# A fused graph-attention layer: the first group's start reordered, head 0's sums called earlier

## The chip, the cores and the metric

The kernel runs on one core of one Trainium2 chip. The metric is the device time of one execution in microseconds, median of several; the profile is that of one execution. The engines are TensorE (PE, matrix products), VectorE (DVE), ScalarE (ACT), GpSimd (POOL) and SyncE (SP); each works through its own queue in order (e1 below moves one instruction in VectorE's queue, and the gap behind it goes). A scheduler, not the program text alone, fixes these orders when the kernel is built: it moves an instruction forward when it believes that its operands are ready.

## The reference, cut to what matters

```python
h = relu(layernorm(x))                     # x: 128 graphs x 64 nodes x 512
# first attention, 4 heads: W_heads[h] 512x512, a_heads[h] 1024
f1, f2 = (h @ W[h]) @ a1[h], (h @ W[h]) @ a2[h]      # "scores"
att = softmax(mask(leaky(f1[:, None] + f2[None, :])))
h1[h] = elu(att @ (h @ W[h]))
# second attention, one head: W_out 2048x512, then a feed-forward layer
o = elu(att2 @ (concat(h1) @ W_out))
y = layernorm(relu(o @ w1 + b1) @ w2 + b2 + o)
out = x + y
```

All in float32. 8192 rows are worked in 16 groups of 512 rows (4 tiles of 128).

## The kernel before: the parts concerned

The 512x512 products are done by a seven-product scheme in place of eight: operand blocks are added and subtracted first ("sums"), and seven products of 256-wide blocks follow (`p` = 1 to 7), whose results are combined by VectorE into `t`, `s15` and the four output blocks. The weights' sums are made once, by GpSimd, and stored in DRAM (`tc`); the data's sums are made for every head and group.

```python
def weight_sums(m):                        # before; m: 4 W_heads, 4 blocks of W_out, w1, w2
    w = MT.pop(m)
    ...
    nc.gpsimd.tensor_tensor(s[0][:, 0], b12, b11, ALU.subtract)          # L202
    nc.gpsimd.tensor_tensor(s[0][:, 1], b22, s[0][:, 0], ALU.subtract)   # L203
    nc.gpsimd.tensor_tensor(s[1][:, 0], b22, b12, ALU.subtract)          # L204
    nc.gpsimd.tensor_tensor(s[1][:, 1], b21, s[0][:, 1], ALU.subtract)   # L205
    ... nc.gpsimd.dma_start(out=TC[m][i], in_=s[i])                      # L208, i = 0, 1

def unit(name, product, post, order): ...
    # after product p: 1 -> s (ScalarE copies the bank), 6 -> t, 5 -> s15 (VectorE, L251);
    # products 7, 3 and 4 add to the banks of 6, 5 and 6, so 7 waits for t, 3 for s15

def scores2(g):                            # second attention's scores, group before
    for j in range(G):                     # 4 tiles x 2: eight products on VectorE, "jf" (L611)
        for c in range(2):
            nc.vector.scalar_tensor_tensor(junk, WH2[g][:, j], 1.0, ao[:, c, :], ..., accum_out=f[...])
    ...

# start-up: fold each head's a into its W (wa = W a), so that scores need no projection
for m in range(FH): fold_dve(m, ab[m])     # heads 0, 1 on VectorE
for m in range(FH, H): fold_pe(m, aT, pw)  # heads 2, 3 on TensorE
...
project_f(0); scores1(0); attn_weights(0 and 1)     # pf, L; s1pe; softmax (L397 to L416)
for m in range(len(mats)): ... weight_sums(m)       # all ten, on GpSimd
run(attend1(0))                            # attention of group 0 (pz, z)
...
for g in range(NG):                        # first projection of g, beside scores2 ... of g - 1
    ...                                    # second projection of g, beside attention of g + 1
```

In the profile, `g_a` is a bank of the first projection, `g_b` of the second, `g_c` and `g_d` of the feed-forward layer. `L` is what ScalarE makes of the folded scores `pf`, `s1pe` the scores of the first attention, `s1e` and `s1A` its softmax, `z` the attention's result, `zs_z` its sums. Line numbers are those of each kernel's own text: the helper of the products `g_a` is L284 before and L300 after, that of `t_a` is L251 and L267, the softmax's subtraction is L404 and L420.

## Time and profile before

| | before |
|---|---|
| device time, median of 3 | 2433.73 us (2433.13 to 2437.04) |
| span of the profiled execution, mean granted clock | 2432.8 us, 0.988 |
| TensorE busy | 2344.2 us, 96% |
| `L` made; softmaxes of the first group | 50.53; 55.13 to 71.74 |
| first product of `g_a` | 81.27 |
| first product of the second projection | 148.79 |
| first product of the next group | 213.16 |

The times are microseconds from the span's start. A timeline line reads: start, duration, engine, line of the text, operation, what it writes <- what it reads, sizes, count; the bracket at its end is the time for which the engine sat idle before it, and what ended that.

### The profile page before, as it was taken

To read this page: it belongs to the slowest core of one execution; us is meant where nothing else is said; L and a number is where in the kernel's file an instruction comes from. 1 tells how busy PE (TensorE), PEld (TensorE's weight loads), DVE (VectorE), ACT (ScalarE), POOL (GpSimd) and SP (SyncE) were. 2 spreads that over 40 slices of the span, in tenths; PEclk is the share of its full clock that TensorE was granted. 3 is DMA by queue.
4 is the path that set the end of the run, shared out by engine and by line. 5 is a ranking of instruction groups with operands and counts; after the bars stand their busy time and mean duration, and the time that the engine had idled before them with its cause. 6 is when DMAs were issued, how large, how long until landed. Compare 5 with 4: busy or idle time off the path is not lost.

```text
span 2432.8 us, 33084 instructions
## 1 busy us (share of the span) xinstructions
PE 2344.2 (96%) x11849; PEld 1961.4 (81%) x11849; DVE 1451.6 (60%) x2468; ACT 787.1 (32%) x1386; POOL 1020.0 (42%) x863
## 2 busy tenths in 40 slices
PE   5799999999999999999999999999999999999997
PEld 4588888888888888888888888888888888888885
DVE  6655565574755647565574755647566574744637
ACT  1342415233251432415233251432415234141412
POOL 6742443534444253443434444253442534433334
PEclk9899999999999999999999999999999999999999
DMA  8644454454544445454454544445454454534542
GB/s 295 235 137 137 129 165 134 139 172 130 169 128 150 157 133 171 130 165 142 135 169 129 168 130 149 156 132 171 130 161 141 135 169 131 164 124 146 166 146 98
DMA packets 260498, 369.00 MB, mean 152 GB/s; under 512 B 22344, under 2 KB 145256, under 8 KB 260336
## 3 DMA queue, kind: packets, MB, share of 16 engines
q1 hardware_dynamic: 252176, 345.92, 44.3%
q10 hardware_dynamic: 5280, 10.49, 1.4%
q0 software_dynamic: 2880, 10.49, 1.1%
q8 instruction: 95, 1.56, 0.3%
q14 instruction: 67, 0.55, 0.1%
HBM read 339.54 MB, written 27.26 MB: 151 GB/s over the span
## 4 chain that ended last, share of the span: by engine, by line
PE 92%; DVE 2%; issue 2%; POOL 2%; DMA 2%; ACT 0%; SPq 0%; DVEq 0%; POOLq 0%; ACTq 0%
PE g_b L299 32%; PE g_a L284 32%; PE g_c L284 8%; PE g_d L299 8%; PE pz L499 4%; PE pa L642 2%; PE pzS L499 1%; PE pto L669 1%; PE pth L348 1%; PE s1pt L449 1%; DMA pw<-in_L_gnn_W_out_dram 1%; PE s1pe L383 1%; PE pf L358 1%; DMA pw<-in_L_gnn_w_dram 0%; DMA aj<-in_adj_dram 0%
## 5 line engine op out<-in xcount | busy, mean ns | idle before, releaser
L299 PE MATMUL g_b<-w,h 128*128 128x256 f32 x2560 | 603.8, 381 | 0.0
L299 PEld LDWEIGHTS g_b<-w,h 128*128 128x128 f32 x2560 | 476.6, 190 | 74.1 <-issue 14.4
L284 PE MATMUL g_a<-zs_z,w 128*128 128x256 f32 x1536 | 376.7, 395 | 41.4 <-issue 31.5
L284 PEld LDWEIGHTS g_a<-zs_z,w 128*128 128x128 f32 x1536 | 304.0, 199 | 98.7 <-issue 43.9
L284 PE MATMUL g_a<-z,w 128*128 128x256 f32 x1536 | 363.1, 379 | 0.0
L284 PEld LDWEIGHTS g_a<-z,w 128*128 128x128 f32 x1536 | 291.6, 190 | 53.0 <-issue 14.7
L299 PE MATMUL g_b<-w,hS 128*128 128x256 f32 x1024 | 243.5, 384 | 0.0
L561 POOL TENSOR_TENSOR hS<-hS,h 128x512 f32<-128x512 f32 x64 | 81.9, 1279 | 384.1 <-DVE hS L523 379.1
L299 PEld LDWEIGHTS g_b<-w,hS 128*128 128x128 f32 x1024 | 189.5, 190 | 38.6 <-issue 10.0
L588 POOL TENSOR_TENSOR h<-h,h 128x512 f32<-128x512 f32 x64 | 81.2, 1270 | 237.7 <-PE g_b L299 237.7
L522 ACT ACTIVATE exc<-exc 128x512 f32<-128x512 f32 x256 | 161.0, 629 | 6.6
L523 DVE SCALAR_TENSOR_TENSOR h<-exc,h 128x512 f32<-128x512 f32 x128 | 107.3, 838 | 62.5 <-ACT exc L522 62.4
L588 POOL TENSOR_TENSOR h<-hS,h 128x512 f32<-128x512 f32 x64 | 81.2, 1269 | 140.1 <-PE g_b L299 138.4
L521 ACT ACTIVATE exc<-h 128x512 f32<-128x512 f32 x128 | 80.7, 631 | 177.4 <-DVE h L558 177.1
L311 POOL TENSOR_TENSOR zs_z<-z,zs_z 128x512 f32<-128x512 f32 x63 | 85.9, 1364 | 111.4 <-PE g_a L284 111.4
L309 POOL TENSOR_TENSOR zs_z<-zS,z 128x512 f32<-128x512 f32 x63 | 89.2, 1417 | 93.0 <-PE g_a L284 72.8
L299 PE MATMUL g_d<-w,rt 128*128 128x256 f32 x512 | 122.5, 382 | 1.8 <-DVE n2ve L324 1.1
L284 PE MATMUL g_c<-ot,w 128*128 128x256 f32 x512 | 121.9, 381 | 0.0
L284 PE MATMUL g_a<-zS,w 128*128 128x256 f32 x512 | 121.1, 379 | 0.0
L310 POOL TENSOR_TENSOR zs_z<-z,zs_z 128x512 f32<-128x512 f32 x63 | 80.2, 1274 | 79.9 <-PE g_d L299 62.1
L299 PEld LDWEIGHTS g_d<-w,rt 128*128 128x128 f32 x512 | 95.9, 190 | 20.5 <-issue 5.2
L284 PEld LDWEIGHTS g_a<-zS,w 128*128 128x128 f32 x512 | 96.0, 190 | 19.0 <-issue 7.4
(155 smaller groups left out, 3659.5 us busy)
## 6 DMA issues: line engine op xcount, KB each, us to landing
w<-tc SPq DMA_DIRECT2D x640, 256.0 KB, 2.7
w<-in_L_gnn_W_heads_dram SPq DMA_DIRECT2D x192, 256.0 KB, 2.8
w<-in_L_gnn_W_out_dram SPq DMA_DIRECT2D x192, 256.0 KB, 2.8
w<-in_L_gnn_w_dram SPq DMA_DIRECT2D x96, 256.0 KB, 2.7
x<-in_x_dram SPq DMA_DIRECT2D x66, 256.0 KB, 2.9
xr<-in_x_dram SPq DMA_DIRECT2D x64, 256.0 KB, 2.9
out_dram<-o SPq DMA_DIRECT2D x64, 256.0 KB, 2.4
tc<-pt POOLq DMA_DIRECT2D x20, 512.0 KB, 6.8
```

What stands on the lines that cost most here:

```text
L284: nc.tensor.matmul(bk[:, o, :], w[:, k, ts(o, P)], a[:, k, :], start=start and o == 0 and k == 0, stop=k == 1, skip_group_check=True,)
L299: nc.tensor.matmul(bk[:, j, :], a[:, k, ts(j, P)], w[:, k, :], start=start and k == 0 and j == 0, stop=i == len(ms) - 1 and k == 1, skip_g ...
L309: eng.tensor_tensor(s2, s1, a11, ALU.subtract)
L310: eng.tensor_tensor(s4, a12, s2, ALU.subtract)
L311: eng.tensor_tensor(s3, a22, s2, ALU.subtract)
L499: nc.tensor.matmul(banks[b][:, c, :].rearrange("p (h n) -> p h n", h=H), src[rows, off + c * P:off + (c + 1) * P], at[rows, b], start=True ...
L521: nc.scalar.activation(ex, src, AF.Relu, scale=-1.0)
L522: nc.scalar.activation(ex, ex, AF.Exp, scale=-1.0)
L523: nc.vector.scalar_tensor_tensor(dst, ex, -1.0, src, ALU.add, ALU.max)
L561: nc.gpsimd.tensor_tensor(dst, dst, H1["22"][:, h], ALU.add)
L588: nc.gpsimd.tensor_tensor(dst[:, h], x0[:, h], x1[:, h], ALU.subtract)
L642: nc.tensor.matmul(pa, AT2[g][:, j, :], WH2[g][:, j, :], start=True, stop=True)
```

## The change

Its title names two things. Head 0's sums of the next group are called during the second projection, in place of at the start of the first. And the first group is rearranged: three heads are folded on VectorE and one on TensorE; the weight sums of heads 0 to 3 come before the softmaxes and all others after them; the sums of W_heads 0 and 1 are read from where GpSimd makes them ("DIRECT") and not by way of DRAM; two products come before the second half of the attention. The mask work on VectorE moves behind the first statistics, and `n1nb`, a small step of the normalisation, moves from VectorE to GpSimd.

```diff
-    homes = ("h11", "h22", "h12", "wh2", "out", "wh2", "out", "wh2", "out", "wh2")
+    homes = ("h11", "h22", "h12", "wh2", "out", "wh2", "out", "wh2", "out", "out")
+    stages = ("ot", "rt", "out", "hS", "ot", "rt", "ot", "rt", "ot", "rt")
...
-    def weight_sums(m):
+    def weight_sums(m, after=None):
...
+        first = nc.gpsimd.tensor_tensor(s[0][:, 0], b12, b11, ALU.subtract)
+        if after is not None:
+            tc.add_manual_dep(first.ins, after.ins.name, ...)
...
-        nc.vector.scalar_tensor_tensor(nb, mean, -1.0, rstd, ALU.mult, ALU.mult)
+        nc.gpsimd.tensor_scalar(nb, mean, rstd, -1.0, ALU.mult, ALU.mult)
...
-            z_sums(g, 0)
...
-    for m in range(FH):
-        fold_dve(m, ab[m])
-    for m in range(FH, H):
-        fold_pe(m, aT, pw)
+    fold_dve(0, ab[0])
+    fold_dve(1, ab[1])
+    fold_pe(2, aT)
+    fold_dve(3, spread_a(3))
+    for m in range(H):
+        weight_sums(m)
     project_f(0)
...
-    for m in range(len(mats)):
-        if m >= H:
-            fetch(m)
-        weight_sums(m)
-    run(attend1(0))
+    attn = attend1(0)
+    for fn in attn[:4]:
+        fn()
+    head0 = project1(0, 0)
+    for fn in head0[:2]:
+        fn()
+    transpose_weights(1)
+    for fn in attn[4:]:
+        fn()
+    z_sums(0, 0)
...
+            side = stage_a(1)
+            for i, m in ((6, 4), (11, 5), (16, 6), (21, 7)):
+                side.insert(i, lambda m=m: more_sums(m))      # fetch(m), weight_sums(m, softmax_end)
...
+            tr, ff, fin = [], [lambda: more_sums(M1), lambda: None, lambda: more_sums(M2), load_rows], []
...
+            early = [lambda: z_sums(g + 1, 0)]
+            at = 8 if g >= 1 else 0
+            run(project2(g), mix(attn, tr) + mix(ff[:at] + early + ff[at:], stage_a(g + 2)) + fin)
```

More of the change, by code (lines that the diff above doesn't have):

```diff
@@ L94, in load @@
         return tl
-    for t in range(G):
+    X[0] = load(0)
+    ar = wk.tile([2 * H, O], FP, tag="elu", name="ar", bufs=3)
+    nc.sync.dma_start(out=ar, in_=a_heads.rearrange("h (r p) -> (h r) p", p=O))
+    for t in range(1, G):
         X[t] = load(t)
+    ah = wk.tile([2 * H * KC, P], FP, tag="elu", name="ah", bufs=3)
+    nc.sync.dma_start(out=ah, in_=a_heads.rearrange("h (r p) -> (h r) p", p=P))
     aj = const.tile([P, N], mybir.dt.int32, name="aj")
@@ L101, in gat_preln_kernel, with masks @@
     negm = const.tile([P, N], FP, name="negm")
-    nc.vector.tensor_scalar(negm, aj, 0.0, None, ALU.is_gt)
-    nc.vector.tensor_scalar(negm, negm, NEG, -NEG, ALU.mult, ALU.add)
     blkones = const.tile([P, NB, N], FP, name="blkones")
-    nc.vector.memset(blkones, 0.0)
-    for b in range(NB):
-        nc.vector.memset(blkones[ts(b, N), b, :], 1.0)
     eye = const.tile([P, N], FP, name="eye")
-    nc.vector.tensor_add(eye, ident[:, 0:N], ident[:, N:2 * N])
-    id32 = const.tile([P, 32], FP, name="id32")
-    nc.vector.tensor_reduce(id32, ident.rearrange("p (j r) -> p r j", r=32), AX.X, ALU.add)
     headrow = const.tile([P, H], FP, name="headrow")
-    nc.vector.tensor_add(headrow, id32[:, 0:H], id32[:, H:2 * H])
     isf = const.tile([P, 2], FP, name="isf")
-    nc.vector.tensor_reduce(isf, id32[:, 0:2 * H].rearrange("p (c h) -> p c h", c=2), AX.X, ALU.add)
     isq = const.tile([P, 2, 2], FP, name="isq")
-    for q in range(2):
-        par = sm.tile([P, 1], FP, tag="par", name=f"par{q}")
-        nc.vector.tensor_reduce(
-            par, ident.rearrange("p (a q r) -> p q a r", a=2, q=2)[:, q], AX.XY, ALU.add
-        )
-        nc.vector.tensor_scalar(isq[:, q], isf, par, None, ALU.mult)
+    wa = const.tile([P, KC, 32], FP, name="wa")
+    def masks():
+        nc.vector.memset(wa, 0.0)
+        id32 = const.tile([P, 32], FP, name="id32")
+        nc.vector.tensor_reduce(id32, ident.rearrange("p (j r) -> p r j", r=32), AX.X, ALU.add)
+        nc.vector.tensor_add(headrow, id32[:, 0:H], id32[:, H:2 * H])
+        nc.vector.tensor_reduce(isf, id32[:, 0:2 * H].rearrange("p (c h) -> p c h", c=2), AX.X, ALU.add)
+        for q in range(2):
+            par = sm.tile([P, 1], FP, tag="par", name=f"par{q}")
+            nc.vector.tensor_reduce(
+                par, ident.rearrange("p (a q r) -> p q a r", a=2, q=2)[:, q], AX.XY, ALU.add
+            )
+            nc.vector.tensor_scalar(isq[:, q], isf, par, None, ALU.mult)
+        nc.vector.memset(blkones, 0.0)
+        for b in range(NB):
+            nc.vector.memset(blkones[ts(b, N), b, :], 1.0)
+        nc.vector.tensor_scalar(negm, aj, 0.0, None, ALU.is_gt)
+        nc.vector.tensor_scalar(negm, negm, NEG, -NEG, ALU.mult, ALU.add)
+        nc.vector.tensor_add(eye, ident[:, 0:N], ident[:, N:2 * N])
     mats = [W_heads[h] for h in range(H)]
@@ L130, in gat_preln_kernel @@
     M1, M2 = 2 * H, 2 * H + 1
-    homes = ("h11", "h22", "h12", "wh2", "out", "wh2", "out", "wh2", "out", "wh2")
+    homes = ("h11", "h22", "h12", "wh2", "out", "wh2", "out", "wh2", "out", "out")
+    stages = ("ot", "rt", "out", "hS", "ot", "rt", "ot", "rt", "ot", "rt")
     MT, TC = {}, {}
-    wa = const.tile([P, KC, 32], FP, name="wa")
-    nc.vector.memset(wa, 0.0)
+    DIRECT = {}
     def fetch(m):
@@ L138, in fetch, with spread_a @@
         nc.scalar.dma_start(out=MT[m], in_=mats[m].rearrange("(k p) o -> p k o", p=P))
-    FH = 2
-    def load_a():
-        ar = wk.tile([2 * H, O], FP, tag="elu", name="ar", bufs=3)
-        nc.sync.dma_start(out=ar, in_=a_heads.rearrange("h (r p) -> (h r) p", p=O))
-        rows = H * 2 * KC
-        ah = wk.tile([rows, P], FP, tag="elu", name="ah", bufs=3)
-        nc.sync.dma_start(out=ah, in_=a_heads.rearrange("h (r p) -> (h r) p", p=P))
-        return ar, ah
-    def spread_a(ar, m):
+    def spread_a(m):
         ab = []
@@ L162, in spread_a, with turn_a @@
         return ab
-    def turn_a(ah):
+    def turn_a():
         rows = H * 2 * KC
@@ L167, in turn_a @@
         nc.tensor.transpose(pt, ah, ident[0:rows, 0:rows])
-        aT = const.tile([P, H, 2, KC], FP, name="aT")
+        aT = wk.tile([P, H, 2, KC], FP, tag="s1", name="aT")
         nc.scalar.copy(aT.rearrange("p h c o -> p (h c o)"), pt)
@@ L180, in fold_dve, with fold_pe @@
                 )
-    def fold_pe(m, aT, pw):
+    def fold_pe(m, aT):
+        pw = aux([P, KC, 2], "pwa")
         for k in range(KC):
@@ L191, in fold_pe @@
                 nc.tensor.matmul(
-                    pw[:, k, :, m - FH], wT[:, o, :], aT[:, m, :, o],
-                    start=(m == FH and k == 0 and o == 0), stop=(o == KC - 1), skip_group_check=True,
-                )
-    def weight_sums(m):
+                    pw[:, k, :], wT[:, o, :], aT[:, m, :, o],
+                    start=(k == 0 and o == 0), stop=(o == KC - 1), skip_group_check=True,
+                )
+        nc.scalar.copy(wa[:, :, m:m + H + 1:H], pw)
+    def weight_sums(m, after=None):
         w = MT.pop(m)
@@ L199, in weight_sums @@
         b21, b22 = w[:, 2:4, 0:Q], w[:, 2:4, Q:O]
-        tag = ("ot", "rt")[m % 2]
-        s = [big.tile([P, 2, 2, Q], FP, tag=f"{tag}{i}", name=f"pt{m}_{i}") for i in range(2)]
-        nc.gpsimd.tensor_tensor(s[0][:, 0], b12, b11, ALU.subtract)
+        tag = stages[m]
+        if tag[1] == "t":
+            s = [big.tile([P, 2, 2, Q], FP, tag=f"{tag}{i}", name=f"pt{m}_{i}") for i in range(2)]
+        else:
+            both = big.tile([P, 2, 2, 2, Q], FP, tag=tag, name=f"pt{m}")
+            s = [both[:, 0], both[:, 1]]
+        first = nc.gpsimd.tensor_tensor(s[0][:, 0], b12, b11, ALU.subtract)
+        if after is not None:
+            tc.add_manual_dep(
+                first.ins, after.ins.name,
+                mybir.DependencyInfo(mybir.DependencyClass.Sync, mybir.DependencyReason.DATA),
+                reason="the sums do not disturb VectorE before",
+            )
         nc.gpsimd.tensor_tensor(s[0][:, 1], b22, s[0][:, 0], ALU.subtract)
@@ L208, in weight_sums @@
             nc.gpsimd.dma_start(out=TC[m][i], in_=s[i])
+        if m < 2:
+            for p, i in ((5, 0), (6, 1), (7, 2), (4, 3)):
+                DIRECT[m, p] = s[i // 2][:, i % 2]
     def piece(m, p):
+        if (m, p) in DIRECT:
+            return DIRECT.pop((m, p))
         w = ring.tile([P, 2, Q], FP, tag="w", name=f"w{m}_{p}")
@@ L415, in softmax @@
             )
-            nc.vector.tensor_copy(A[:, :, H], A[:, :, 0])
+            LAST["A"] = nc.vector.tensor_copy(A[:, :, H], A[:, :, 0])
             return A
@@ L433, in softmax @@
         return A
-    A1, E1 = {}, {}
+    A1, E1, LAST = {}, {}, {}
     def attn_weights(p):
@@ L540, in project1 @@
         z = ZB[g]
+        first = (g, h) == (0, 0)
         if h == 0:
@@ L544, in project1 @@
                 H1[b] = big.tile([P, H, 2, T], FP, tag=tag, name=f"h{b}_{g}")
-            z_sums(g, 0)
-        s2, s3, s4 = ZSUM[h]
-        blk = {1: z["11"][:, h], 2: z["12"][:, h], 3: s4, 4: z["22"][:, h],
-               5: z["S1"][:, h], 6: s2, 7: s3}
+        sums = {6: 0, 7: 1, 3: 2}
+        blk = {1: "11", 2: "12", 4: "22", 5: "S1"}
         def post(what, a, b=None):
@@ L561, in post @@
                 nc.gpsimd.tensor_tensor(dst, dst, H1["22"][:, h], ALU.add)
-        s = unit(f"a{g}_{h}", product_t(h, lambda p: blk[p]), post, (1, 6, 5, 2, 7, 3, 4))
+        s = unit(
+            f"a{g}_{h}", product_t(h, lambda p: ZSUM[h][sums[p]] if p in sums else z[blk[p]][:, h]),
+            post, (1, 2, 6, 5, 7, 3, 4) if first else (1, 6, 5, 2, 7, 3, 4),
+        )
         def next_sums():
@@ L726, in mix @@
     def mix(*lists):
+        lists = [l for l in lists if l]
         keyed = [((i + 0.5) / len(l), n, fn) for n, l in enumerate(lists) for i, fn in enumerate(l)]
         return [fn for _, _, fn in sorted(keyed, key=lambda k: k[:2])]
-    ar, ah = load_a()
     for m in range(H):
@@ L736, in gat_preln_kernel @@
         norm1(t)
-    ab = [spread_a(ar, m) for m in range(FH)]
-    aT = turn_a(ah)
+    masks()
+    ab = {m: spread_a(m) for m in (0, 1)}
+    aT = turn_a()
     for t in range(G):
         transpose_h(t)
-    for m in range(FH):
-        fold_dve(m, ab[m])
-    pw = aux([P, KC, 2, H - FH], "pwa")
-    for m in range(FH, H):
-        fold_pe(m, aT, pw)
-    for c in range(2):
-        nc.vector.tensor_copy(wa[:, :, c * H + FH:(c + 1) * H], pw[:, :, c])
+    fold_dve(0, ab[0])
[4 more added lines that the diff above has]
+        weight_sums(m)
     project_f(0)
@@ L751, in gat_preln_kernel @@
         attn_weights(p)
-    for p in range(2):
-        transpose_weights(p)
-    for m in range(len(mats)):
-        if m >= H:
-            fetch(m)
-        weight_sums(m)
-    run(attend1(0))
+    softmax_end = LAST["A"]
+    transpose_weights(0)
+    attn = attend1(0)
[8 more added lines that the diff above has]
+    z_sums(0, 0)
     ao = const.tile([P, 2, FO], FP, name="ao")
@@ L763, in gat_preln_kernel, with load_rows, more_sums @@
     bs = const.tile([P, FO], FP, name="bs")
-    rows = [(ao[:, 0, :], a_out[0:FO]), (ao[:, 1, :], a_out[FO:2 * FO]), (b2s, b2), (gs, gamma), (bs, beta)]
-    for dst, src in rows:
-        nc.sync.dma_start(out=dst, in_=src[None, :].to_broadcast([P, FO]))
     b1s = const.tile([P, DF // P], FP, name="b1s")
-    for d in range(DF // P):
-        nc.sync.dma_start(out=b1s[:, d:d + 1], in_=b1[ts(d, P)][:, None])
+    def load_rows():
+        rows = [(ao[:, 0, :], a_out[0:FO]), (ao[:, 1, :], a_out[FO:2 * FO]), (b2s, b2), (gs, gamma), (bs, beta)]
+        for dst, src in rows:
+            nc.sync.dma_start(out=dst, in_=src[None, :].to_broadcast([P, FO]))
+        for d in range(DF // P):
+            nc.sync.dma_start(out=b1s[:, d:d + 1], in_=b1[ts(d, P)][:, None])
+    def more_sums(m):
+        fetch(m)
+        weight_sums(m, softmax_end)
     for t in range(G, 2 * G):
@@ L773, in gat_preln_kernel @@
     for g in range(NG):
-        heads = [fn for h in range(H) for fn in [lambda h=h: steps.extend(project1(g, h))]]
-        side = stage_e(g - 1) if g >= 1 else stage_a(1)
-        steps, n = [], 6 * H
-        done = 0
+        if g >= 1:
+            side = stage_e(g - 1)
+        else:
+            side = stage_a(1)
+            for i, m in ((6, 4), (11, 5), (16, 6), (21, 7)):
+                side.insert(i, lambda m=m: more_sums(m))
+        done, n = 0, 6 * H
         for i in range(n):
             if i % 6 == 0:
-                heads[i // 6]()
-            steps[i]()
+                steps = head0 if (g, i) == (0, 0) else project1(g, i // 6)
+            if (g, i // 2) != (0, 0):
+                steps[i % 6]()
             while done * n < (i + 1) * len(side):
@@ L789, in gat_preln_kernel @@
         else:
-            tr, ff, fin = [], [], []
+            tr, ff, fin = [], [lambda: more_sums(M1), lambda: None, lambda: more_sums(M2), load_rows], []
         if g < NG - 1:
-            tail = mix(ff, stage_a(g + 2)) if ff or g + 2 < NG else []
-            run(project2(g), mix(attn, tr) + tail + fin if attn or tr else tail + fin)
-        else:
-            held = 2
-            run(project2(g), tr + [lambda: None] * 6 + ff[:held])
-            left = ff[held:]
-            run(left, [
+            early = [lambda: z_sums(g + 1, 0)]
+            at = 8 if g >= 1 else 0
+            run(project2(g), mix(attn, tr) + mix(ff[:at] + early + ff[at:], stage_a(g + 2)) + fin)
+        else:
+            run(project2(g), tr + [lambda: None] * 6 + ff[:2])
+            run(ff[2:], [
                 lambda: scores2(g), lambda: None, lambda: None, lambda: None, lambda: softmax2(g),
```

## The prediction

> **What bounds the kernel now.** I read the page's busy shares first, then its 40 slices, then the list of waits of TensorE, then the timeline around the places where it waits.
>
> ```profile
> PE 2344.2 (96%) x11849; PEld 1961.4 (81%) x11849; DVE 1451.6 (60%) x2468; ACT 787.1 (32%) x1386; POOL 1020.0 (42%) x863
> PE   5799999999999999999999999999999999999997
> PEclk9899999999999999999999999999999999999999
> ```
>
> TensorE is busy 2344.2 of 2432.8 us; 88.6 us are idle. A slice is 60.8 us: the first two, at 5 and 7 tenths, hold about half of that, the rest is spread thinly. So two things can be won: the start-up, and small gaps that come back in every group. The change takes no product away. The waits, largest first, name both:
>
> ```profile
> PE g_a L284 <- issue: 31.5, 14, 3.5
> PE pab L158 <- DMA ar<-in_L_gnn_a_heads_dram: 12.7, 1, 12.7
> PE s1pt L449 <- DVE s1A L412: 10.7, 2, 9.4
> PE g_a L284 <- DVE t_a L251: 7.8, 1, 7.8
> ```
>
> The columns are total, times, longest. The first line is one gap of about 2.2 us at the start of each of the last 14 groups. The title of the change suggests that these are waits for head 0's sums (L309 to L311 on GpSimd). The timeline at one of them says otherwise:
>
> ```profile
> 347.37 1.26 POOL L311 TENSOR_TENSOR zs_z<-z,zs_z 128x512 f32<-128x512 f32 x1
> ...
> 363.26 0.68 DVE L320 BATCH_NORM_STATS2 n1st<-x 128x6 f32<-128x512 f32 x1
> 364.19 0.68 DVE L251 TENSOR_TENSOR t_a<-g_a,s_a 128x512 f32<-128x512 f32 x1
> 364.97 5.38 PE L284 MATMUL g_a<-zs_z,w 128*128 128x256 f32 x16 [2.28 <-issue]
> ```
>
> The last sum of head 0 ended at 348.63, before the group's first product at 355.62. TensorE started again 0.10 us after VectorE's t_a (364.19 + 0.68 = 364.87). At the gaps near 511, 656 and 802 us it is again 0.10 us. t_a stood in VectorE's queue behind scores2's eight products (L611) and a normalisation, solid work since 342.93.
>
> The start-up in order of time:
>
> ```profile
> 57.96 4.05 DVE L404 TENSOR_TENSOR s1e<-s1e,s1mx 128x512 f32<-128x512 f32 x1
> 65.98 0.69 DVE L403 TENSOR_REDUCE s1mx<-s1e 128x8 f32<-128x512 f32 x1
> 81.27 1.99 PE L284 MATMUL g_a<-z,w 128*128 128x256 f32 x8
> 88.61 4.36 DVE L310 TENSOR_TENSOR zs_z<-z,zs_z 128x512 f32<-128x512 f32 x1
> 98.20 3.78 PE L284 MATMUL g_a<-zs_z,w 128*128 128x256 f32 x8 [7.85 <-DVE t_a L251]
> ```
>
> Folding ends at 48.4, scores reach VectorE at 55.1, the two softmaxes end at 71.7, the first product is at 81.3, TensorE is steadily full from about 118, and the second projection starts at 148.95. The 4.05 and 4.36 us operations are of a kind that takes about 0.7 elsewhere; GpSimd was then subtracting weights (1.26 us an operation).
>
> **What the Trainium skill says.** "SBUF — State Buffer", section Who interferes with whom: VectorE operations with two SBUF inputs share a read port with GpSimd, held for the whole instruction; the other side blocks. The trace agrees: 4.05 us against 0.92 for L404 of the second softmax; reductions stay at 0.69. "TensorE: Matmul & The Clock Gate", section Architectural detail, says ScalarE and VectorE queues are strict FIFO; t_a behind scores2 agrees, and it will matter for ScalarE below. The same page, section What's actually happening, says an idle array falls to half clock; granted clock was 0.66 at 90 to 100 us, and the product at 98.20 (x8: four matmuls in two passes) took 3.78, twice the usual 1.89 us.
>
> **The change part by part.**
>
> *Steady groups: 0 us.* I built both programs and compared the order on each engine. GpSimd's order per group is the same except for four n1nb that move to it from VectorE (about 0.5 us each at n1rs's length; on VectorE about 0.16). Head 0's sums stand where they stood: the scheduler had already moved them up. VectorE's 95 instructions around the boundary keep their order; t_a remains behind scores2. TensorE's feed-forward products move by one place among the second projection's. So I expect the 14 gaps to remain, near 31 us. The removed n1nb lie beside the products.
>
> *Folding: −8.5 us.* VectorE's mask work now comes after the statistics; six of these operations each cost one GpSimd operation of 1.26 us, from about 13.5 when the mask lands, so folding starts near 21 (before: 22.55). Twenty-four folds at 0.61 us (23.16 to 23.77 is one) are 14.7, ending near 36 instead of 48.4; TensorE has one head to turn, not two, and isn't last. But the new buffers give part back: W_out's first block (home "out") takes the buffer in which head 2's sums are staged, so ScalarE, in order, issues that load ahead of L only after those sums were stored. GpSimd gets to that store near 34.3; stores take 6.8 us (page, median), more in this crowded time: L near 42, before 50.53.
>
> *Softmax undisturbed: −5.6 us.* 55.13 to 71.74 is 16.6. Without GpSimd's subtractions one takes seven operations at 0.72, two short ones at 0.22 to 0.24 and ScalarE's 0.63, less overlap: about 5.5, two are 11.0.
>
> *Products before the second half of attention, sums of heads 0 and 1 read where they are made: −11 us.* From the softmax's end to the end of the next group's pf, with nine products done, the kernel before took 111.5 − 71.7 = 39.8. Followed through the new queues at the durations above, the first product comes some 2 us after the softmax rather than 9.5, the 7.85 wait goes (the zs operations no longer meet a train of weight sums), and a wait of about 5 us comes in its place while the evictions of zS and z22 stand behind the first elu: about 29.
>
> *Weight sums of heads 4 to 7 during the first projection: +9.4 us.* Their loads stand in ScalarE's queue, each waiting for GpSimd to finish the previous block in the same buffer: block 4 done after head 0's last product (near 87 on the new clock), block 6 landing 8 us later (the chain of before shows such loads at 7.9 to 10.3), four subtractions of 1.26, then the load of w1, 8 more, then the end of block 5 before block 7's load may start. While ScalarE waits, s1 copies, Exp and elus wait, and VectorE behind them. I get TensorE waits of 3.6 at head 2's second product, 1.3 at a later one and 6.3 at head 3's second; the kernel before had 1.8 there. 11.2 − 1.8 = 9.4. The last blocks are stored near 137 and needed near 150, so the second projection isn't held up.
>
> Sum: −8.5 −5.6 −11 +9.4 = −15.7. 2433.7 − 15.7 = 2418.0 us.
>
> **The rivals.** (a) The gaps go too: if the moved feed-forward products let VectorE reach t_a 2 us earlier, 31 us more are won and the time is about 2387. For it: VectorE waited for TensorE before 342.93. Against: the order of its last 95 instructions is the same, and so are the products that it waits for. (b) ScalarE's queue doesn't hold TensorE up, because loads land in 5 us when fewer stores run: the 9.4 vanish, 2408. For it: ScalarE is only 32% busy. Against: it is in order, and the loads wait on GpSimd, not on bytes. (c) The start is bound by bytes: 300 to 390 GB/s until 50 us, and the new order brings seven weight pieces forward; x6 and x7 then come late for VectorE's queue ahead of the scores, or the stores of block 2 take 10 us or more. Folding's gain falls to 3 and later loads slip: about 2427. (d) The last weights come too late for the second projection: up to 10 us more, 2428.
>
> **Range and chances.** Nothing in 2280 us of steady groups should move; all uncertainty is in the first 150 us, where the gain lies between 5 and 29. Range 2405 to 2429. Faster by over 2% needs 48.7 us, which only (a) with a full start-up gain gives: 3%. Slower by 2%: 1%. Within: 96%.
>
> **What will show it.** First product of g_a near 60 (before 81.3); L404 near 0.7; the second projection's first product near 133 (before 148.95); ScalarE idle behind loads of W_out near 91 to 100 and 103 to 115, with TensorE gaps at s1's heads 2 and 3; 14 gaps of about 2 us still there, each 0.1 us after a t_a. I'm wrong if those gaps are gone, or if the second projection starts before 122 or after 144.

## The result, and the profile after

| | before | after |
|---|---|---|
| device time, median | 2434.19 us (2433.13 to 2437.04, 4 runs) | 2413.73 us (2407.63 to 2418.43, 4 runs) |
| ratio, 95% interval | | 0.9913 (0.9889 to 0.9937): within 2% |
| span of the profiled execution, clock | 2432.8 us, 0.988 | 2411.1 us, 0.984 |

Every ratio in this text is the mean time of one kernel's fast runs over the mean of the other's fast runs of the same rounds, so it is not quite the ratio of the medians.

First the page of the changed kernel: busy time of each engine, and TensorE's busy share and granted clock in 40 slices of 60.3 us.

```profile
PE 2331.4 (97%) x11805; PEld 1949.1 (81%) x11805; DVE 1433.7 (59%) x2418; ACT 782.5 (32%) x1383; POOL 1051.0 (44%) x927
...
PE   6899999999999999999999999999999999999997
...
PEclk7999999999999999999999999999999999999999
```

The second slice went from 7 to 8 tenths busy; the rest of TensorE's line looks as before. The first digit of the clock fell from 9 to 7: the granted clock was 0.73 from 20 to 30 us and 0.50 from 30 to 55, where the folding of one head on TensorE (29.02 to 36.01) and both softmaxes lie. The waits of TensorE name what is left (total, times, longest):

```profile
PE g_a L300 <- issue: 29.1, 14, 3.2
PE g_a L300 <- ACT s_a L265: 10.8, 2, 6.3
```

The 14 gaps at the group boundaries are still there: 29.1 us against 31.5. The second line is new. One of the gaps, in the timeline:

```profile
345.99 0.68 DVE L336 BATCH_NORM_STATS2 n1st<-x 128x6 f32<-128x512 f32 x1
...
346.60 0.40 DVE L635 TENSOR_TENSOR s2dg<-eye,f 128x256 f32<-128x256 f32 x1
346.92 0.68 DVE L267 TENSOR_TENSOR t_a<-g_a,s_a 128x512 f32<-128x512 f32 x1
...
347.70 5.38 PE L300 MATMUL g_a<-zs_z,w 128*128 128x256 f32 x16 [1.96 <-issue]
```

`t_a` ended at 347.60, TensorE went on 0.10 us later, as before. It stood behind the same work: scores2's products, a normalisation, `s2dg`. The sums of this group's head 0 were finished at 331.68 (GpSimd's last of them started at 330.42 and took 1.26 us), 16 us ahead of the gap. So the call that the title names first had nothing to take away there.

The sixteen matmuls after this gap took 5.38 us, at a granted clock of 0.50 from 349 to 351 us; sixteen at full clock take 3.69. The granted clock isn't the same after every gap: the slow form follows 11 of the 14 gaps in the profile of before and 9 of 14 in that of after. Adding gap and slow part, before spends 31.5 + 18.2 us at the boundaries and after 29.1 + 16.1; the difference of 4.5 us is nearly all of what the two traces differ by beyond the start. (From the next group's first product to the end: before 2432.8 − 213.16 = 2219.6, after 2411.1 − 196.20 = 2214.9.)

The start, from the timeline:

```profile
38.81 0.46 ACT L380 ACTIVATE L<-pf,isq 128x128 f32<-128x128 f32 x1 [2.59 <-POOL pt L216]
...
45.64 0.69 DVE L420 TENSOR_TENSOR s1e<-s1e,s1mx 128x512 f32<-128x512 f32 x1
...
56.64 1.97 PE L300 MATMUL g_a<-z,w 128*128 128x256 f32 x8
...
101.31 0.37 ACTq L147 DMA_DIRECT2D pw<-in_L_gnn_w_dram  x1
101.73 0.63 ACT L421 ACTIVATE s1e<-s1e 128x512 f32<-128x512 f32 x1 [10.91 <-POOL pt L216]
...
103.40 3.47 PE L300 MATMUL g_a<-z,w 128*128 128x256 f32 x8 [6.26 <-ACT s_a L265]
```

`L` comes 11.7 us earlier, the softmax's subtraction takes 0.69 us in place of 4.05, the first product comes 24.6 us earlier. Then something is given back: ScalarE issued the load of w1 at 101.31 and had stood idle for 10.91 us before its next operation, until GpSimd had finished the block in the same buffer; `s_a` waited behind it, and TensorE 6.26 us for `s_a`. The same happens again 19 us later (12.55 and 4.56 us). In stages, each worked out from the times at which it starts and ends:

| stage (us) | before | after | difference | predicted |
|---|---|---|---|---|
| start to `L` | 50.53 | 38.81 | −11.7 | −8.5 |
| `L` to the softmax | 4.60 | 4.66 | +0.1 | 0 |
| two softmaxes | 16.61 | 11.46 | −5.1 | −5.6 |
| softmax's end to nine products done | 39.8 | 27.0 | −12.8 | −11 |
| from there to the second projection | 37.3 | 50.3 | +13.0 | +9.4 |
| second projection's first product | 148.79 | 132.23 | −16.6 | −15.7 |

### The profile page after: what moved, and what is told of

It is laid out like the page before. It is cut to its first block, busy times and chain, and to the rows that moved or that the text cites. A ratio compares the mean times of both kernels' runs of the same rounds, so it can differ in the third digit from the quotient of the medians.

```text
span 2411.1 us, 32917 instructions
## 1 busy us (share of the span) xinstructions
PE 2331.4 (97%) x11805; PEld 1949.1 (81%) x11805; DVE 1433.7 (59%) x2418; ACT 782.5 (32%) x1383; POOL 1051.0 (44%) x927
## 4 chain that ended last, share of the span: by engine, by line
PE 93%; POOL 2%; issue 2%; DVE 1%; DMA 1%; ACT 0%; ACTq 0%; SPq 0%; DVEq 0%; POOLq 0%
PE g_b L315 33%; PE g_a L300 31%; PE g_d L315 8%; PE g_c L300 8%; PE pz L515 4%; PE pa L660 2%; PE pzS L515 1%; PE pto L687 1%; PE s1pt L465 1%; PE pth L364 1%; PE s1pe L399 1%; PE pf L374 1%; DMA pw<-in_L_gnn_W_out_dram 0%; POOL pt L216 0%; POOL pt L207 0%
## 5 line engine op out<-in xcount | busy, mean ns | idle before, releaser
L300 PE MATMUL g_a<-zs_z,w 128*128 128x256 f32 x1504 | 364.9, 393 | 29.1 <-issue 29.1
L300 PE MATMUL g_a<-z,w 128*128 128x256 f32 x1520 | 362.0, 381 | 11.4 <-ACT s_a L265 10.8
L300 PEld LDWEIGHTS g_a<-zs_z,w 128*128 128x128 f32 x1504 | 295.6, 197 | 84.0 <-issue 41.8
L606 POOL TENSOR_TENSOR h<-h,h 128x512 f32<-128x512 f32 x64 | 86.8, 1356 | 225.2 <-PE g_b L315 225.2
L327 POOL TENSOR_TENSOR zs_z<-z,zs_z 128x512 f32<-128x512 f32 x63 | 85.9, 1363 | 108.9 <-PE g_a L300 108.9
L326 POOL TENSOR_TENSOR zs_z<-z,zs_z 128x512 f32<-128x512 f32 x63 | 85.2, 1353 | 91.7 <-PE g_d L315 73.8
```

The lines of the kernel that those rows point to most:

```text
L300: nc.tensor.matmul(bk[:, o, :], w[:, k, ts(o, P)], a[:, k, :], start=start and o == 0 and k == 0, stop=k == 1, skip_group_check=True,)
L326: eng.tensor_tensor(s4, a12, s2, ALU.subtract)
L327: eng.tensor_tensor(s3, a22, s2, ALU.subtract)
L606: nc.gpsimd.tensor_tensor(dst[:, h], x0[:, h], x1[:, h], ALU.subtract)
```

## The experiments

Each was timed beside the kernel before on one chip. "gaps" is the line "g_a <- issue" of TensorE's waits, mostly the boundaries; the next group's first product is a clean measure of the start, as the kernels with an unchanged start show: 196.20 after, 196.17, 195.28 and 196.04 in e1, e3 and e5.

| run | median us | before there | ratio (95%) | second projection | next group | gaps |
|---|---|---|---|---|---|---|
| e1 | 2392.68 | 2435.97 | 0.9818 (0.9805 to 0.9831) | 131.61 | 196.17 | 2.9 |
| e2 | 2410.04 | 2435.97 | 0.9894 (0.9881 to 0.9906) | 147.78 | 212.16 | 1.9 |
| e3 | 2420.28 | 2435.97 | 0.9933 (0.9922 to 0.9945) | 131.31 | 195.28 | 30.9 |
| e4 | 2422.19 | 2435.97 | 0.9941 (0.9929 to 0.9953) | 119.81 | 198.44 | 32.8 |
| e5 | 2370.47 | 2439.69 | 0.9715 (0.9701 to 0.9730) | 132.07 | 196.04 | 1.1 |
| e6 | 2410.74 | 2439.69 | 0.9885 (0.9869 to 0.9901) | 118.58 | 182.56 | 34.6 |
| e7 | 2419.64 | 2439.69 | 0.9918 (0.9901 to 0.9934) | 134.83 | 198.81 | 33.2 |
| e8 | 2414.43 | 2439.69 | 0.9898 (0.9877 to 0.9919) | 127.44 | 191.65 | 35.4 |
| e9 | 2360.54 | 2439.92 | 0.9675 (0.9661 to 0.9690) | 120.51 | 184.48 | 2.3 |
| e10 | 2449.25 | 2439.92 | 1.0041 (1.0026 to 1.0056) | 157.80 | 222.18 | 39.2 |
| e11 | 2430.45 | 2439.92 | 0.9969 (0.9952 to 0.9986) | 139.75 | 203.73 | 31.1 |
| e12 | 2429.91 | 2439.92 | 0.9962 (0.9947 to 0.9977) | 137.93 | 201.90 | 35.9 |

### What makes the 14 gaps: e1, e2, e3, e5

**e1: t_a goes first.** The call alone can't be moved, since the scheduler puts scores2 where its operands are ready; a dependency is needed.

```diff
-            [lambda: scores2(g)] + gap * 6 + ...
+            gap * 3 + [lambda: scores2(g, TA[6])] + gap * 3 + ...      # TA[6]: t_a of the next group's head 0
...                                                                     # in scores2, for (j, c) == (2, 0):
+                    tc.add_manual_dep(jf.ins, after.ins.name, ...)     # products of tiles 2, 3 wait for t_a
```

> The changed kernel, with the second half of scores2's products (tiles 2 and 3) told to wait for t_a of the next group's head 0, so that t_a goes first in VectorE's queue. Theory (the 14 gaps are t_a standing behind scores2): they go, all or nearly all of 29.1 us, and with them most of the slow sixteen matmuls after a gap (5.38 us instead of 3.69 in 10 of 14 groups, some 17 us); 2414 becomes about 2372, between 2362 and 2390. Rival (the gaps are waits for the sums of head 0 on GpSimd, as the title has it, or any wait of TensorE's own): unchanged, 2409 to 2419.

The gaps went from 29.1 to 2.9 us, as the theory has it, and the rival is out. But the time fell to 2392.7 and not to 2372, outside the range given: a new wait had come. First TensorE's waits of e1, then its timeline:

```profile
PE g_a L300 <- DVE s_a L267: 16.6, 13, 1.5
...
PE g_a L300 <- issue: 2.9, 5, 0.8
```

```profile
358.83 1.89 PE L300 MATMUL g_a<-zs_z,w 128*128 128x256 f32 x8
...
360.22 0.69 DVE L443 TENSOR_TENSOR s2A<-s2e,s2rb 128x512 f32<-128x512 f32 x1
360.83 0.69 DVE L539 SCALAR_TENSOR_TENSOR hS<-exc,hS 128x512 f32<-128x512 f32 x1
361.43 0.68 DVE L267 TENSOR_TENSOR s_a<-g_a,s_a 128x512 f32<-128x512 f32 x1
...
362.17 1.99 PE L300 MATMUL g_a<-zs_z,w 128*128 128x256 f32 x8 [1.45 <-DVE s_a L267]
```

`s_a` of head 1 stands behind softmax2 in VectorE's queue. It isn't later than before: it starts at 361.43, in the changed kernel at 361.40, both in groups that begin at about 338.65. But TensorE, without the gap of 1.96 us and the slow matmuls behind it, begins the product ahead of this wait at 358.83 in place of 361.98. After these waits of about 1.45 us eight matmuls take 1.99 us, which is full speed.

**e2: the same edit on the kernel before.**

> The same one edit on the kernel before. Theory: the gaps don't depend on the change, so it wins as much here: 31.5 us of gaps and some 18 us of slow products, 2434 becomes about 2386 (2375 to 2405), with the start-up untouched, second projection's first product still near 149. Rival (the gaps of before were waits for the late sums of head 0, which the change moves): unchanged, near 2434.

Gaps 1.9 us in place of 31.5, and the same new wait, 17.8 us in 15 places. The ratio is 0.9894: the repair wins as much as the whole change did, with the old start (148 and 212). It missed its range (2375 to 2405) for the same reason as e1. The gaps were in the kernel before for the same reason as after, and don't depend on the change.

**e3: head 0's sums called late again.**

```diff
+            if g >= 1:
+                z_sums(g, 0)          # at the start of project1, h == 0
-            early = [lambda: z_sums(g + 1, 0)]
+            early = []
```

> The changed kernel with the sums of head 0 of groups 1 to 15 called again where the kernel before calls them (at the start of the group's first projection). Theory: they are not on the path, since GpSimd's order hardly moves: within 5 us of the changed kernel's 2414. Rival (the moved sums are what the change won in the steady groups): each of 15 groups loses up to the 3.8 us that three sums take, up to 57 us, at least 20 us slower.

0.9933 beside the changed kernel's 0.9913, with overlapping intervals, and 30.9 us of gaps beside 29.1. The difference of the ratios is 4.9 us (that of the medians, from two sets of rounds, 6.6), at the edge of the 5 us that the theory allowed. The rival's 20 us aren't there: the part of the change that its title names first does nothing that these runs can show.

**e5: s_a goes first too.** e1, and:

```diff
-            ... + gap * 3 + [lambda: softmax2(g)] + gap * 6
+            ... + gap * 5 + [lambda: softmax2(g, TA[5])] + gap * 4     # TA[5]: s_a of head 1
...                                                                     # in softmax, the sum after Exp:
+            tc.add_manual_dep(red.ins, after.ins.name, ...)
```

> The kernel of e1_ta_first, with softmax2 called two steps later and the part of it that follows Exp told to wait for s_a of head 1. Theory (in e1, VectorE's queue had moved the wait: s_a of head 1 stood behind softmax2, 13 times 1.3 us): these 16.6 us go too; e1's 2392.7 becomes about 2376, between 2369 and 2384. Rival (softmax2 is now late for its own readers, the transposes and the second attention, and TensorE waits there): 2388 to 2397.

2370.5 us, as expected. In two stretches of 500 us in the middle (the columns are TensorE, its weight loads, VectorE, ScalarE and GpSimd busy, then granted clock, DMA share and GB/s), the changed kernel and then e5:

```profile
500.00:1000.00 500.00, 492.83 (x2502) 411.51 (x2501) 300.27 (x497) 176.53 (x311) 210.32 (x185) 0.99 0.44 146
1000.00:1500.00 500.00, 494.23 (x2545) 415.60 (x2544) 302.36 (x491) 158.75 (x283) 218.69 (x186) 0.99 0.44 147
```

```profile
500.00:1000.00 500.00, 499.23 (x2562) 417.20 (x2561) 313.06 (x500) 179.60 (x317) 221.21 (x192) 1.00 0.47 149
1000.00:1500.00 500.00, 499.65 (x2581) 421.60 (x2580) 322.49 (x529) 160.57 (x286) 222.71 (x186) 1.00 0.49 154
```

TensorE is busy all but 1.1 of 1000 us, against 12.9, and gets its full clock. From the next group's start to the end e5 takes 2365.2 − 196.04 = 2169.2 us, 45.7 less than the changed kernel. Of these the gaps are 29.1 − 1.1 = 28.0 and the slow matmuls after them 16.1: a gap of 2 us cost 3.2 on average.

### What held TensorE up in the first projection: e4, e6

**e4: the loads on GpSimd's queue.**

```diff
-        nc.scalar.dma_start(out=MT[m], in_=mats[m]...)
+        eng = nc.scalar if m < H else nc.gpsimd
+        eng.dma_start(out=MT[m], in_=mats[m]...)
```

> The changed kernel with the loads of W_out, w1 and w2 issued from GpSimd's queue in place of ScalarE's. Theory (ScalarE, in order, stood 11 and 12 us behind loads that waited for GpSimd, and held up s_a and so TensorE): the two gaps of 10.8 us in the first projection and the slow products after them (2.7 us) go, the second projection starts near 120 in place of 132; but GpSimd now waits for loads itself and the last blocks may be late there, so between 2401 and 2412. Rival 1 (the loads' bytes or GpSimd's own work are the limit): 2414 within 2. Rival 2 (last blocks late): the first projection wins 10 and the second loses as much, with TensorE waits on weight pieces of g_b near 130 to 150.

The first half came true to the microsecond: TensorE's waits for ScalarE's `s_a` are gone, and the second projection starts at 119.81, 12.4 us earlier. Then all of it was lost, and the next group starts 2.2 us later than in the changed kernel. Rival 2 was right that it would be lost, not how. From e4's timeline:

```profile
134.24 1.26 POOL L208 TENSOR_TENSOR pt<-pw 128x512 f32<-128x512 f32 x1 [7.43 <-DMA pw<-in_L_gnn_w_dram]
...
137.06 0.69 DVE L337 BATCH_NORM_STATS2 n1st<-x 128x6 f32<-128x512 f32 x1 [9.76 <-DMA x<-in_x_dram]
...
138.40 3.78 PE L316 MATMUL g_b<-w,hS 128*128 128x256 f32 x8 [5.80 <-DVE z L528]
...
144.84 0.18 DVE L339 BATCH_NORM_AGGREGATE n1mv<-n1st 128x2 f32<-128x6 f32 x1 [6.50 <-POOL n1nb L351]
```

VectorE waited 9.76 us for rows of x, which SyncE had issued behind weight pieces that were not stored yet, and then 6.50 us for GpSimd, which had itself waited 7.43 us for w2 and was working off what stood behind that. The eviction of `z` stood behind both, and TensorE behind the eviction.

**e6: w1 and w2 later.** As e4, and:

```diff
-            tr, ff, fin = [], [lambda: more_sums(M1), lambda: None, lambda: more_sums(M2), load_rows], []
+            tr, ff, fin = [], [load_rows], [lambda: fetch(M1, TA[5]), lambda: weight_sums(M1, TA["c22"])]
...
+            if g == 1:
+                side.insert(9, lambda: fetch(M2))
+                side.insert(16, lambda: weight_sums(M2, TA[5]))
```

> As e4_loads_on_gpsimd, with the loads and sums of w1 and w2 moved out of the first group's first projection, to behind the second projection and into the next group. Theory (in e4 the first projection won 12.4 us, and VectorE and GpSimd then stood behind the load of w2 and a late x, 8.7 us and slow products): the second projection starts near 120 and is no longer held up, the next group starts near 185 (changed kernel 196.4), in all 2402, between 2397 and 2409. Rival (W_out's last blocks are late by themselves): the next group starts at 194 or later, 2411 or more.

Now nothing holds the second projection up. The next group starts at 182.56, 13.6 us earlier than in the changed kernel, so ScalarE's queue and w1's and w2's early place were worth that much. W_out's last blocks aren't late by themselves. The total, 2410.7, lies just above the range given and shows only half of it: 0.9885 beside 0.9913 is 6.8 us. The trace has the other half in the boundaries, 34.6 us of gaps with the slow form after 12 of 14. These two numbers differ from run to run in kernels whose steady groups are alike, and I can't say what sets them.

### The terms of the start: e7, e10, e12, e8, e11

**e7: GpSimd busy during the softmaxes.**

```diff
+            for i in range(10 if t == 0 else 0):       # after the first masked sum
+                junk = wk.tile([P, F], FP, tag="t", name=f"junk{i}")
+                op = nc.gpsimd.tensor_tensor(junk, HN[0], HN[0], ALU.subtract)
```

> The changed kernel with ten useless subtractions on GpSimd (128x512, results thrown away) while VectorE does the two softmaxes of the first group. Theory (the softmaxes of before were slowed by GpSimd's subtractions, which the change moves out): they take 16 us or more in place of 11.0, single operations 4 us, the first product of g_a comes 4 to 7 us later (56.6 becomes 61 to 64) and the next group as much, 2414 becomes 2419 with the scatter of the gaps. Rival (the softmaxes were slow for another reason, such as the loads): operations stay at 0.69 us, no change.

The ten subtractions ran from 44.61 to 57.40, all through the softmaxes, and these took 12.65 us (43.83 to 56.48) in place of 11.46. No operation took over 0.95 us. The next group came 2.6 us later. That is less than the theory said and more than the rival.

**e10: the kernel before with GpSimd quiet.** Weight sums from the third block on wait for the end of the softmaxes.

```diff
+        weight_sums(m, LAST["A"] if m >= 2 else None)
```

> The kernel before, with GpSimd's weight sums from the third block on held back until the first group's softmaxes are done. Theory (it is these subtractions that slow the softmaxes there): L404's 4.05 us becomes 0.69, the two softmaxes take 11.0 to 11.5 us in place of 16.6 (start of the first masked sum to the last copy). Rival (e7's useless subtractions hardly slowed them, so something else did, such as the loads): 15 us or more, with operations of over 2 us. The total says little, since all weight sums come later: 2434 to 2455.

From e10's timeline, the first masked sum, the subtraction that took 4.05 us in before, and the last copy:

```profile
50.38 0.69 DVE L409 TENSOR_TENSOR s1e<-s1pe,negm 128x512 f32<-128x512 f32 x1 [2.16 <-PE s1pe L395]
...
52.56 0.69 DVE L416 TENSOR_TENSOR s1e<-s1e,s1mx 128x512 f32<-128x512 f32 x1
...
61.62 0.22 DVE L428 COPY s1A<-s1A 128x128 f32<-128x128 f32 x1
```

The softmaxes take 11.46 us, as in the changed kernel to the hundredth. Holding the sums back also holds back their stores and the loads behind them: e10 moved no bytes in these 11.46 us, before 253 GB/s in its 16.61. But the changed kernel moved 303 GB/s in its 11.46 us, so it isn't the bytes. GpSimd's weight sums did slow the softmaxes by 5.1 us. The whole kernel is slower, as expected, since all later sums come later: the order costs more elsewhere unless the rest is rearranged too.

**e12: e7 with two different inputs and four result buffers.**

```diff
-                op = nc.gpsimd.tensor_tensor(junk, HN[0], HN[0], ALU.subtract)
+                op = nc.gpsimd.tensor_tensor(junk, HN[0], HN[1], ALU.subtract)   # buffers "t" and "s15" in turn
```

> As e7_busy_softmax, but each useless subtraction reads two different tiles, and the results go to four buffers in turn. Theory (in e7 VectorE was hardly delayed since both inputs were one tile, or each operation waited for the one before): the softmaxes take 14 us or more and one operation 2.5 us or more. Rival (GpSimd's subtractions as such don't slow them that much): 11 to 12 us, as in e7 (12.7 with its copy).

The scheduler put some of the subtractions ahead of the softmaxes. There, in e12's timeline, one VectorE operation was held up by far longer than any in before:

```profile
39.43 6.04 DVE L385 TENSOR_TENSOR R<-U,headrow 128x512 f32<-128x512 f32 x1
...
40.00 4.92 POOL L416 TENSOR_TENSOR junk<-hn,hn 128x512 f32<-128x512 f32 x4
...
44.89 1.53 POOL L342 TENSOR_TENSOR n1rs<-n1ve,mhalf 128x1 f32<-128x1 f32 x2
```

`R`, which takes 0.68 us undisturbed, took 6.04 and ended only after four subtractions, when GpSimd had gone on to its small operations. The softmaxes start 4.4 us later than in the changed kernel (47.86 for 43.47) and take 2.1 us longer; the next group is 5.7 us late. In the softmaxes themselves (13.5 us from 47.86 to 61.40) the worst operation took 1.25 us, so the theory's 2.5 us for one of them isn't there, and the change of inputs did not bring it. So such a subtraction can hold a VectorE operation for the length of several GpSimd instructions, or not at all. What decides it is left open.

**e8: the attention whole before the first products.** The two calls are swapped.

```diff
-    for fn in head0[:2]:
-        fn()
     transpose_weights(1)
     for fn in attn[4:]:
         fn()
+    for fn in head0[:2]:
+        fn()
```

> The changed kernel with the first group's attention done whole before its first two products. Theory (two products done between the halves use a wait): the first product of g_a comes at 63 to 66 in place of 56.6, some 3 us of this last, the second projection starts at 134 to 137 in place of 132.2. Rival (TensorE waits for the second half anyway and the order gives nothing): 132 to 133. In the total either is within 5 us of 2414.

Both were wrong: without the early products the start is better. From e8's timeline, the first product of the first and of the second projection:

```profile
60.89 1.99 PE L300 MATMUL g_a<-z,w 128*128 128x256 f32 x8
...
127.44 1.89 PE L315 MATMUL g_b<-w,h 128*128 128x256 f32 x8
```

The first product is 4.3 us later than in the changed kernel, but nine products are done at 79.67, 25.6 us after the softmaxes' end at 54.07, where the changed kernel needs 27.0. The waits behind the loads are then shorter too (7.2 us in place of 10.8). The next group starts 4.6 us earlier; 0.9 of that was there before the edit could act. The total can't show this, with 35.4 us of gaps.

**e11: two heads folded on TensorE again.**

```diff
-    fold_dve(3, spread_a(3))
+    fold_pe(3, aT)
```

> The changed kernel with head 3 folded on TensorE again (two heads there, two on VectorE), as in the kernel before. Theory (TensorE's transposes and copies through ScalarE are the longer way; one head ended at 36.0 there): the last fold ends 9 to 12 us later, L near 48 in place of 38.8, all of it carried to the first product of g_a (66 in place of 56.6) and to the next group's start, in all 2423. Rival (ScalarE's wait for the load and GpSimd's stores set L, not the folding): L by 42, under 4 us lost.

`L` comes at 44.74, 5.9 us later, between theory and rival; it now waits for TensorE's `pf` and not for the load. The next group is 7.5 us later. So folding a third head on VectorE is worth some 6 to 7.5 us here; the 5.8 us that are left of the 11.7 up to `L` are mostly the earlier start of the folding (18.14 for 22.55, 4.4 us).

### e9: what the experiments point to

e5, e6 and e8 together.

> e5 (t_a and s_a first), e6 (loads of W_out, w1 and w2 on GpSimd's queue, w1 and w2 late) and e8 (attention whole first) in one kernel. Theory (independent parts: the 14 gaps; 13.6 us of start, which e6 showed at the next group's first product, 182.6 for 196.2; a few us of e8): 2370.5 less 13.6 and less 0 to 4, 2355, between 2347 and 2362; the next group's first product near 180. Rival (the start's gain is lost again later, as e6's total of 2410.7 for 2414 suggests; or GpSimd's queue and the gap's repair disturb one another): 2366 or more.

2360.5 us, ratio 0.9675, faster than both kernels and than e5 (0.9715). From its timeline, the first product of the second projection and of the next group:

```profile
120.51 1.89 PE L328 MATMUL g_b<-w,h 128*128 128x256 f32 x8
...
184.48 1.89 PE L313 MATMUL g_a<-z,w 128*128 128x256 f32 x8
```

The start is 11.6 us earlier than e5's, not 13.6 to 17.6: it is 1.9 later than e6's, so e8's order seems to add nothing once ScalarE's queue is clear; part of its gain had been shorter waits there. e6 with e8's order alone was not run. The next groups pass with 2.3 us of gaps.

## Why the prediction was right, and where its steps were off

The predicted 2418.0 us lies 4.3 us above the measured 2413.7, and the range held. Step by step:

**Steady groups, 0 us: right.** 14 gaps, 29.1 us, each 0.1 us after a `t_a`, for the reason given; e1 and e2 show the reason, e3 that the moved sums do nothing that shows. Rival (a) is out. What the step did not contain is the scatter: the half clock after a gap comes after 9 to 13 of 14 gaps, and with the gaps' own lengths this moved the two profiles apart by 4.5 us. The changed kernel's four runs spread over 10.8 us. The prediction priced a gap at its idle time alone; e5 shows that it costs 3.2 us and not 2.

**Folding, −8.5: right in kind, measured −11.7.** Folding started at 18.14 (predicted 21) and `L` came at 38.81 (42). ScalarE did wait for the store of head 2's sums, but 2.59 us only: the load behind that store was issued at 38.31, not near 41. TensorE's one head, called "not last", ended at 36.0 after VectorE's folds (32.8).

**Softmax undisturbed, −5.6: right, −5.1.** e10 gives the cause, by quieting GpSimd in the kernel before. e7 and e12 show that the effect isn't a fixed price.

**Products before the second half of attention, −11: the size was near (−12.8), the cause wrong.** This is the step that failed. e8 takes the early products away and the stretch gets 1.4 us shorter, not longer. Nor did the wait of about 5 us come that the step put in the place of the 7.85: TensorE was idle for 1.4 us of this stretch, in before for 9.0. e8 shows where the gain lies: its first product comes 6.8 us after the softmaxes (before 9.5), and from there nine products take 18.8 us in place of 30.2. The wait of 7.85 us for `t_a` and the half clock behind it are gone; in before `t_a` stood in VectorE's queue behind `zs_z` (4.36 us) and `n1nb` (3.03 us for two), while GpSimd was busy. What is left as a cause are the other parts of the change: no weight sums on GpSimd while the `zs_z` are made, the first sums read where they are made, and `n1nb` moved off VectorE. These weren't separated.

**Weight sums in the first projection, +9.4: right in mechanism, too small.** TensorE waited 6.3 and 4.6 us where 3.6, 1.3 and 6.3 were predicted: 10.8 in place of 11.2 (and in before 1.2, not 1.8). The slow products after the two waits, 3.47 and 3.02 us in place of 1.89 each, weren't counted, and the stretch lost 13.0. e4 and e6 confirm ScalarE's queue as the holder (rival (b) is out). Rivals (c) and (d) did not occur: `L` was early, and nothing in the second projection waited for weights.

Errors of −3.2, +0.5, −1.8 and +3.6 us cancelled in the sum, by luck: −16.6 for −15.7. (The second projection of before starts at 148.79 in the trace; the prediction's 148.95 was misread.) The medians differ by 20.5 us, the two profiles by 21.7; in the profiles the rest lies at the boundaries.

## What to carry to other kernels

When TensorE pauses once per group, look at which instruction ended just before it resumed and at what stood ahead of that one in its queue, before believing that a late operand is at fault; here the operand had been ready for 16 us, and ordering two VectorE instructions won more than the whole rearrangement. After such a repair look again, because the wait tends to move to the next instruction in line. A load that waits for a buffer stops every computation behind it in the queue that issues it (here for 10.91 and 12.55 us), and a price read in one trace, such as an operation slowed by its neighbour, is not constant.

## What the Trainium skill lacked or had wrong

- "TensorE: Matmul & The Clock Gate", section What's actually happening, puts the fall to half clock after at least one idle window of some 3.4 us, and its section Why this matters for your kernels allows gaps up to about 3 us. In the changed kernel 12 of the 14 boundary gaps lasted 1.8 to 2.0 us, and after 7 of these 12 sixteen matmuls took 5.38 us in place of 3.69. After e1's waits of about 1.4 us none did. That it varies fits the page's remark that the window runs freely; the threshold doesn't fit.
- "SBUF — State Buffer", section Who interferes with whom, has the shared ports locked for a whole instruction by whichever of the two engines issued first. Here a VectorE operation was held over several GpSimd instructions in a row: 6.04 us in place of 0.68 over four subtractions (e12), 4.05 in place of 0.69 in the kernel before. In e7 an operation of the same kind ran in 0.69 us in the middle of ten subtractions. The page doesn't say when a waiting operation is let in.
- "DMA: Bandwidth & Descriptors", section Issuing engines are not separate DMA queues, says that issuing from several engines saves only the time to initiate a transfer. It doesn't weigh a load that must first wait for its buffer, where the choice of engine decides whose computations wait with it: moving six loads from ScalarE to GpSimd started the second projection 12.4 us earlier (e4).
